# S of the spectral mix: computed in the mix, or beside the forward transform and loaded

## Chip, cores, metric

One Trainium2 chip, one core. The metric is the device time of one launch in microseconds; the median of several runs counts.

## The reference

The input x is (16, 16, 256, 256): 16 images of 16 channels. Layer 0, which holds the change, is a Laplace neural operator on the group-normalized input: with `alpha` the 2D Fourier transform of an image and four complex poles per axis and channel pair (i, k),

```
A  = 1 / (omega1 - weights_pole1)            # (row frequency o, i, k, p)
Bm = 1 / (omega2 - weights_pole2)            # (column frequency x, i, k, q)
S  = einsum('ikpq,oikp,xikq->oxik', weights_residue, A, Bm)
output_residue1 = einsum('biox,oxik->bkox', alpha, S)      # the mix
x1 = ifft2(output_residue1).real
C  = einsum('biox,oikp->bikpx', alpha, A)                  # and a second part by the poles,
D  = einsum('bikpx,xikq->bikpq', C, Bm)                    # which gives x2
x  = x + x1 + x2 / (Nx * Ny)
```

S is the same for all images. Layer 1 (convolutions with a kernel made from the data, Mish, a gate) follows and is not touched.

## The kernel before

Everything is float32. Four stages follow each other: `layer0_forward` (to 1377 us), `layer0_mix` (to 2907), `layer0_back` (to 3560) and `layer1` (to the end).

**Forward.** 64 steps (b, cg): 16 images by 4 groups of 4 channels. A step does `rows` twice (L207 transform along the rows into the PSUM tile `pu`, L214 the part by poles into `pv`), `poles` (L241) and, from the second image on, `columns` for the image before (L313 into the PSUM tile `px`, emptied by ACT at L320 with a scale, sent to the DRAM tensor `al` by DMAs on POOL's queue, L329). `pu` and `px` have two buffers each, of one bank. ACT copies half of `pu` to `right` (L222) and DVE forms sum and difference (L224). `halves` makes the group norm of the next step by two small matmuls (L34, L42) and DVE operations between them. PE's order is the program's, written out by hand; the other engines' order is set by the framework's planner from its own costs, so their work can run ahead of the program where its inputs and buffers allow.

From step 4 on, each step also advances the generator `tables` (L383) by one piece. There are 43: 16 pieces of T, one per output channel k (the residues times Bm: DVE L415 to L431, four matmuls L437, ACT's copy L445, a write to the DRAM tensor `td`), 11 pieces of three groups each of the poles A (DVE L466 to L490, written to `avd`), and 16 of exponentials for the last part (DVE L515 to L534, ACT's Sin L523, written to `ed`).

**Mix.** 33 groups g of four row frequencies. For each: `load_poles` and `load_spectrum` bring A and alpha; `poles` (L629) spreads A into block-diagonal weights `lt`; `residues` (L643) multiplies them with T, which lies in SBUF as `tt`, in 64 matmuls, and S goes from PSUM into the tile `s` by 8 copies on DVE (L651) and 8 on ACT (L653). `spread` (L605 on ACT, L607 on DVE) writes alpha into the tile `alb`, block-diagonal too. `mix` multiplies 256 column frequencies (L665), ACT empties (L672) into `y`. Four times f: `turn` transposes (L681), `columns` goes back along the columns (L700), ACT copies the odd half (L709), DVE forms sum and difference (L712, L713), and POOL's queue writes to `hd` (L720). `s`, `alb` and `y` are single tiles: S and the spread of group g+1 are made in the four turns of group g, after the mix of g has read the old ones, in this order per turn:

```
yt = turn(y, f)
if f == 3: spread(spectrum, f)
for k0 in range(2 if f == 0 else 4 * f, 4 * f + 4, 2): residues(lt, s, k0)
if f < 3: spread(spectrum, f)
if g + 2 < NF: (f == 0: av = load_poles(g + 2)); spectrum[f] = load_spectrum(g + 2, f)
between = columns(g, f, yt)
```

In the mix the order of PE, ACT, DVE and POOL is written out by hand; the loads are issued on SP's queue, in the order in which they stand in the program.

Of the kernel before, what the change touches and what calls it, by code (L numbers as in the profile page):

```python
# [10 lines left out]
F32 = mybir.dt.float32  # L11
# [61 lines left out]
def layer0_forward(ctx, tc, d, al, bd, tabs):  # L73
# [262 lines left out]
    with tc.manual_schedule(engines={mybir.EngineType.PE}):  # L336
# [4 lines left out]
        pieces = tables(ctx, tc, d, psx, tabs)  # L341
        acc = rsc = None
        for i, (b, cg) in enumerate(steps):
# [16 lines left out]
            if b:  # L360
                for g0 in range(8 * cg, 8 * cg + 8 if cg < 3 else NF, 4):
                    columns(b - 1, g0, rsc)
            if i + 2 < len(steps):
                fetched.append(fetch(*steps[i + 2]))
            if i >= 4:
                next(pieces, None)
# [16 lines left out]
def tables(ctx, tc, d, psum, tabs):  # L383

    nc = tc.nc
    td, avd, ed = tabs
# [3 lines left out]

    krow = load(nc, cp, d["krow_t"], [P, N], "krow_t")
    w = frequencies(nc, cp, d["tx"], krow, [P, N], "wt")
# [18 lines left out]
    for k in range(C):  # L411
        e = tp.tile([P, N], F32, tag="te", name="te")
        r = tp.tile([P, N], F32, tag="trec", name="trec")
        br = tp.tile([P, N], F32, tag="tbr", name="tbr")
# [7 lines left out]
        for h in range(2):  # L422
            wt = tp.tile([P, 2, 2, 16, M], F32, tag=f"wt{h}", name="wt")
            shape = [P, 16, M]
            for part, c, coef in ((0, 0, rr), (0, 1, ri), (1, 0, nri), (1, 1, rr)):
                nc.vector.tensor_tensor(
                    wt[:, part, c],
                    mt[:, h].unsqueeze(2).to_broadcast(shape),
                    coef[:, k].unsqueeze(1).to_broadcast(shape),
                    ALU.mult,  # L430
                )  # L431
            wts.append(wt)
        yield
        ps = psum.tile([P, 2, N], F32, tag="px", name="pt")
        for h, wt in enumerate(wts):
            for part, rhs in ((0, br), (1, e)):
                nc.tensor.matmul(  # L437
                    ps[:, h],
                    lhsT=wt[:, part].rearrange("p c i m -> p (c i m)"),
# [4 lines left out]
        t = tp.tile([P, 2, N], F32, tag="tt", name="tt")  # L444
        nc.scalar.copy(t, ps)  # L445
        nc.sync.dma_start(out=td[:, :, k], in_=t)

    krow = load(nc, cp, d["krow_m"], [P, N], "krow_m")  # L450
    w = frequencies(nc, cp, d["ty"], krow, [P, N], "wm")
    sign = load(nc, cp, d["sign_m"], [P, 1], "sign_m")
    pr = cp.tile([P, 32], F32, name="tpr")
    pi = cp.tile([P, 32], F32, name="tpi")
    for q in range(4):
        nc.sync.dma_start(out=pr[32 * q : 32 * q + 32], in_=d["p1r_ip"])
        nc.sync.dma_start(out=pi[32 * q : 32 * q + 32], in_=d["p1i_ip"])
    nc.vector.tensor_scalar(pi, pi, sign, None, ALU.mult)
    pr2 = cp.tile([P, 32], F32, name="tpr2")
    nc.vector.tensor_tensor(pr2, pr, pr, ALU.mult)  # L460
    npr = cp.tile([P, 32], F32, name="tnpr")
    nc.vector.tensor_scalar(npr, pr, -1.0, None, ALU.mult)
    for g in range(NF):
        four = [P, 32, 4]
        e = tp.tile(four, F32, tag="ae", name="ae")
        nc.vector.tensor_tensor(  # L466
            e,
            w[:, 4 * g : 4 * g + 4].unsqueeze(1).to_broadcast(four),
            pi.unsqueeze(2).to_broadcast(four),
            ALU.add,  # L470
        )
        r = tp.tile(four, F32, tag="ar", name="ar")
        nc.vector.tensor_tensor(r, e, e, ALU.mult)
        nc.vector.tensor_tensor(r, r, pr2.unsqueeze(2).to_broadcast(four), ALU.add)
        nc.vector.reciprocal(r, r)
        av = tp.tile([P, 32, 4, 3], F32, tag="av", name="av")
        half = [64, 32, 4]
        nprb = npr.unsqueeze(2)
        nc.vector.tensor_tensor(av[:64, :, :, 1], r[:64], nprb[:64].to_broadcast(half), ALU.mult)
        nc.vector.tensor_tensor(av[64:, :, :, 1], r[64:], e[64:], ALU.mult)  # L480
        nc.vector.scalar_tensor_tensor(
            av[:64, :, :, 0].rearrange("p k f -> p (k f)"),
            e[:64].rearrange("p k f -> p (k f)"),
            -1.0,
            r[:64].rearrange("p k f -> p (k f)"),
            ALU.mult,
            ALU.mult,
        )
        nc.vector.tensor_tensor(av[64:, :, :, 0], r[64:], nprb[64:].to_broadcast(half), ALU.mult)
        nc.vector.tensor_scalar(av[:, :, :, 2], av[:, :, :, 0], -1.0, None, ALU.mult)  # L490
        nc.sync.dma_start(out=avd[g], in_=av.rearrange("p k f l -> p (k f l)"))
        if g % 3 == 2:
            yield


    phase = load(nc, cp, d["phase"], [P, 1], "phase")
    turn = cp.tile([P, 1], F32, name="turn")
    nc.vector.tensor_scalar(turn, phase, TWO_PI, None, ALU.mult)
    last = load(nc, cp, d["last"], [P, 1], "last")
    c1 = 6.28125  # L500
    c2 = float(np.float32(TWO_PI - c1))
    for i, axis in enumerate("12"):
        pr = cp.tile([P, C], F32, name=f"epr{axis}")
        pi = cp.tile([P, C], F32, name=f"epi{axis}")
        for a in range(2):
# [1028 lines left out]
```

## Time and profile before

| | us |
|---|---|
| median of 3 runs (7282.32 to 7289.96) | 7288.94 |
| the profiled execution | 7272.96 |
| its span | 7271.2 |
| forward: from the start to its last ACT copy | 1377.5 |
| mix: to the last group's end | 1529.7 |
| layer0_back, layer1 | 652.8, 3711 |

| engine | busy in the whole span |
|---|---|
| PE (weight loads) | 91% (50%) |
| DVE | 77% |
| ACT | 53% |
| POOL | 48% |

A row of the profile's groups names line, engine, operation, output<-inputs, shapes and count, then busy time and mean duration, then the engine's idle time before these instructions and what ended it. A float32 matmul is recorded as two instructions. A timeline row is start, duration, engine, line, operation, and in brackets the idle time before it. A wait row is the waiting engine and line, the releaser, then the sum in us, the number and the longest.

### The profile page before, as it was taken

The page shows a single profiled execution, that of the slowest core. Times are in us where ns is not written, and L with a number is a line of the kernel's source. Part 1 is how long each engine was busy: PE and PEld are TensorE (multiplying, and loading weights), DVE is VectorE, ACT ScalarE, POOL GpSimd, SP SyncE. Part 2 cuts the span into 40 slices and gives each one's busy share as a digit, 9 for nine tenths or more (in the row PEclk, how much of TensorE's full clock was granted, in tenths as well). Part 3 has the DMA queues.
Part 4 walks back from the last instruction along what each step waited for, and adds up shares of the span by engine and source line. Part 5 has one row for each costly group of instructions (what it writes and reads, how often), then busy time and mean ns, then how long its engine had stood idle before and what let it go on. Part 6 is the DMA issues. An engine that isn't in the chain of part 4 may idle for free.

```text
span 7271.2 us, 144305 instructions
## 1 busy us (share of the span) xinstructions
PE 6603.5 (91%) x55592; PEld 3651.8 (50%) x55592; DVE 5587.6 (77%) x10106; ACT 3876.9 (53%) x6043; POOL 3524.5 (48%) x4614
## 2 busy tenths in 40 slices
PE   7889999899999998999789999999999999999996
PEld 5767778666666766677423333333333333333332
DVE  8999985466666666788678787788877887778875
ACT  2223333466666665222366666666666666666662
POOL 2334445322222222666555666556665566665663
PEclk9899999999999999999889999999999999999999
DMA  3334444433333332999767888888888889888886
GB/s 100 114 112 125 123 120 125 123 99 99 99 96 99 98 99 87 325 325 326 242 180 225 254 269 249 254 261 258 271 244 252 256 254 275 253 247 260 253 261 229
DMA packets 716081, 1443.39 MB, mean 199 GB/s; under 512 B 98954, under 2 KB 525254, under 8 KB 673638
## 3 DMA queue, kind: packets, MB, share of 16 engines
q1 hardware_dynamic: 567206, 959.76, 44.1%
q0 software_dynamic: 148192, 474.40, 21.1%
q8 instruction: 444, 7.27, 0.4%
q14 instruction: 239, 1.96, 0.1%
HBM read 877.12 MB, written 556.47 MB: 197 GB/s over the span
## 4 chain that ended last, share of the span: by engine, by line
PE 37%; DMA 5%; ACT 4%; DVE 3%; issue 1%; POOL 0%; SPq 0%; DVEq 0%; ACTq 0%; POOLq 0%
PE c2ps L1185 14%; PE c L1037 11%; PE pd L1105 10%; ACT wide L1085 3%; DMA rows<-cf 3%; DVE top L1116 1%; PE pr L1064 1%; DMA z<-zn 1%; DVE t L1113 1%; DMA cf<-bot 0%; SPq L1017 0%; DVE pair L1175 0%; ACT L1085 0%; ACT bot L1056 0%; POOL o L1253 0%
## 5 line engine op out<-in xcount | busy, mean ns | idle before, releaser
L1085 ACT ACTIVATE wide<-c,b 32x512 f32<-32x512 f32 x2176 | 1479.0, 680 | 832.1 <-PE c L1037 768.3
L1116 DVE TENSOR_TENSOR top<-pd,t 32x512 f32<-32x512 f32 x2176 | 1504.1, 691 | 53.0 <-DMA cf<-top 0.5
L1037 PE MATMUL c<-z,w 102*128 102x512 f32 x2048 | 1046.0, 636 | 212.3 <-ACT wide L1085 190.8
L1097 POOL COPY wide<-wide 32x1031 f32<-32x1031 f32 (+1 forms) x576 | 576.0, 1000 | 1167.8 <-ACT wide L1085 1141.7
L1113 DVE TENSOR_TENSOR t<-pd,r 64x512 f32<-64x512 f32 x1088 | 744.5, 684 | 504.5 <-PE pd L1105 472.1
L1105 PE MATMUL pd<-wide,dw 128*128 128x512 f32 x2048 | 1026.4, 622 | 16.4 <-DVE top L1116 11.5
L720 POOL DMA_DIRECT2D hd<-h x512 | 324.4, 640 | 1195.9 <-DVE h L713 1170.9
L1037 PEld LDWEIGHTS c<-z,w 102*128 102x128 f32 x2048 | 384.0, 197 | 818.3 <-issue 488.8
L1185 PE MATMUL c2ps<-rows,c 128*32 128x512 f32 x6144 | 722.9, 603 | 24.6 <-DMA rows<-cf 19.0
L1105 PEld LDWEIGHTS pd<-wide,dw 128*128 128x128 f32 x2048 | 370.3, 194 | 641.6 <-issue 490.5
L1098 POOL COPY wide<-wide 32x1031 f32<-32x1031 f32 (+1 forms) x576 | 573.3, 995 | 33.7
L643 PE MATMUL ps<-tt,lt 128*64 128x256 f32 x4224 | 495.5, 384 | 13.8 <-DMA tt<-td 10.6
L700 PE MATMUL ph<-ix,yt 64*128 64x256 f32 x4128 | 500.9, 390 | 5.6 <-issue 4.8
L313 PE MATMUL px<-wxn,u 128*64 128x256 f32 x4224 | 481.7, 379 | 7.8 <-ACT o L320 7.8
L207 PE MATMUL pu<-fy,eo 128*128 128x128 f32 x2048 | 427.0, 292 | 26.5 <-DVE u L224 21.8
L1185 PEld LDWEIGHTS c2ps<-rows,c 128*32 128x32 f32 x6144 | 176.7, 109 | 533.5 <-issue 400.3
L700 PEld LDWEIGHTS ph<-ix,yt 64*128 64x128 f32 x4128 | 392.3, 190 | 92.0 <-issue 45.0
L873 POOL TENSOR_TENSOR x<-x,o 128x512 f32<-128x512 f32 x256 | 324.3, 1267 | 216.6 <-DVE o L872 197.3
L607 DVE TENSOR_SCALAR alb<-alc,m 128x1024 f32<-128x1024 f32 x330 | 420.2, 1398 | 0.0
L214 PE MATMUL pv<-at,eo 128*128 128x128 f32 x2048 | 413.7, 285 | 0.0
L651 DVE COPY s<-ps 128x512 f32<-128x512 f32 x264 | 265.7, 1024 | 189.0 <-PE ps L643 171.2
L665 PE MATMUL pg<-alb,s 128*32 128x64 f32 x16896 | 274.1, 221 | 132.3 <-issue 86.4
(217 smaller groups left out, 11785.6 us busy)
## 6 DMA issues: line engine op xcount, KB each, us to landing
rows<-cf SPq DMA_DIRECT2D x128, 2176.0 KB
z<-zn SPq DMA_DIRECT2D x768, 257.8 KB
cf<-top POOLq DMA_DIRECT2D x512, 240.0 KB, 7.0
cf<-bot POOLq DMA_DIRECT2D x96, 840.0 KB, 11.4
alc<-al SPq DMA_DIRECT2D x264, 256.0 KB
zn<-zb SPq DMA_DIRECT2D x128, 516.0 KB
o<-zn SPq DMA_DIRECT2D x128, 516.0 KB
z<-in_x SPq DMA_DIRECT2D x64, 1024.0 KB
```

What stands on the lines that cost most here:

```text
L207: nc.tensor.matmul(pu[:, xh, e].rearrange("p v m -> p (v m)"), lhsT=lhs, rhs=fy[:, e], start=True, stop=True,)
L313: nc.tensor.matmul(ps[64 * k : 64 * k + 64, :, h], lhsT=u[:, h, part, g0 + j + k].rearrange("p f c -> p (f c)"), rhs=wxn[:, h, part], star ...
L643: nc.tensor.matmul(ps[64 * h : 64 * h + 64, v], lhsT=lt[:, h, k, 1 - v : 3 - v].rearrange("p l f c -> p (l f c)"), rhs=tt[:, h, k], start= ...
L700: nc.tensor.matmul(ph[q][:, e], lhsT=yt[lanes, i].rearrange("p t k -> p (t k)"), rhs=ix[lanes, i], start=n == 0, stop=n == 3,)
L1037: nc.tensor.matmul(ps[:, a], lhsT=w, rhs=z[:k, c : c + 2, 0:N], start=True, stop=True)
L1085: nc.scalar.activation(self.feat[64 - 32 * q : 96 - 32 * q, f, self.groups[g], :H], ps[q][32 * f : 32 * f + 32], AF.Mish, bias=b1[0][32 * ...
L1097: nc.gpsimd.tensor_copy(flat[0:32, f, 1:m], flat[64:96, f, 0 : m - 1])
L1098: nc.gpsimd.tensor_copy(flat[96:128, f, 0 : m - 1], flat[32:64, f, 1:m])
L1105: nc.tensor.matmul(ps, lhsT=dwt if self.tail else dw, rhs=self.feat[:, f, cs, :H], start=True, stop=True,)
L1113: nc.vector.tensor_tensor(t[64:128], ps[:64], self.r[:, cs], ALU.mult)
L1116: nc.vector.tensor_tensor(self.top[32 * f : 32 * f + 32, cs, q], ps[lanes], t[lanes], ALU.add)
L1185: nc.tensor.matmul(ps[32 * j : 32 * j + 32], lhsT=w[:, blk], rhs=src[:, 4 * j + blk : 4 * j + blk + 4, x : x + H], start=(i, blk) == (0, 0 ...
```

## The change

T is no longer kept in DRAM, nor the poles. `tables` now computes S itself: for each pair of output channels (8 pairs), `first` makes T as before for each of the two (into an SBUF tile), `second(k, h)` makes A for 8 of the input channels as a block operand `a` of four quarters of 32 rows each (DVE and ACT), `products` multiplies each quarter of `a` with the same quarter of T, so four operands on 32 rows of the array, each into a PSUM bank of its own, and ACT copies the four banks into `s` tiles (three buffers), each written to the new DRAM tensor `sd` by a DMA on SP's queue. The four banks are the two buffers of `px` and the two of `pu`. `last_products` does the 33rd group, with 64 lanes a bank. One channel pair is 14 pieces, with two exponentials among them 16; 128 in all. They are taken twice a step from the second image on (`columns`, piece, `columns`, piece), three times in the steps with cg = 3. `frequencies` can write in place, and tables share buffers by tags.

In the mix, `poles`, `residues` and T in SBUF are gone. `load_residues_of(g, v)` loads S of a group from `sd` as a tile `raw` of 128 x 4096 (three buffers): once straight (v = 0, one DMA) and once with real and imaginary parts exchanged (v = 1, two DMAs of 64 partitions each). `fill` turns 32 column frequencies of it into `s`: DVE the v = 0 half with a sign per lane, ACT the v = 1 half. Eight fills stand where the eight pairs of `residues` stood. `load_spectrum` is one DMA of 128 partitions instead of two of 64, and lane order and constant masks follow.

```diff
@@ layer0_forward
-        pieces = tables(ctx, tc, d, psx, tabs)
+        pieces = tables(ctx, tc, d, (psx, psu), tabs)
             if b:
                 for g0 in range(8 * cg, 8 * cg + 8 if cg < 3 else NF, 4):
                     columns(b - 1, g0, rsc)
+                    if g0 in (8 * cg, 28):
+                        next(pieces, None)
             if i + 2 < len(steps):
                 fetched.append(fetch(*steps[i + 2]))
-            if i >= 4:
+            if b:
                 next(pieces, None)
@@ tables
+    a = cp.tile([P, 2, 2, 36, 2, 4], F32, name="ta")
+    nc.gpsimd.memset(a, 0.0)
+    def second(k, h):
+        two = [P, 2, 132]
+        e = tp.tile(two, F32, tag="arg", name="ae")
+        nc.vector.tensor_tensor(e, wm..., pi..., ALU.add)
+        r = tp.tile(two, F32, tag="exp_n", name="ar")
+        nc.vector.tensor_tensor(r, e, e, ALU.mult)
+        nc.vector.tensor_tensor(r, r, pr2..., ALU.add)
+        nc.vector.reciprocal(r, r)
+        for v in range(2):
+            t = tp.tile(two, F32, tag="n" if v else "exp_b", name="ax")
+            for j in range(2):
+                nc.scalar.activation(t[:, j], e[:, j], AF.Identity, bias=xc..., scale=xs...)
+            nc.vector.tensor_tensor(t, t, r, ALU.mult)
+            for c in range(2):
+                nc.scalar.activation(a[:, :, c, :33, v], t..., AF.Copy, scale=mc[:, c : c + 1])
+    def banks():
+        return [
+            (psx if r < 2 else psu).tile([P, 2, N], F32, tag="px" if r < 2 else "pu", name="s")
+            for r in range(4)
+        ]
+    def evict(ps, n=P):
+        t = tp.tile([P, 2, N], F32, tag="s", name="s", bufs=3)
+        nc.scalar.copy(t[:n], ps[:n])
+        return t.rearrange("p k x -> p (k x)")
+    def products(k, tt, h, c, g0):
+        ps = banks()
+        for j in range(2):
+            for r in range(4):
+                q = slice(32 * r, 32 * r + 32)
+                nc.tensor.matmul(
+                    ps[r][:, j],
+                    lhsT=a[q, j, c, g0 : g0 + 16].rearrange("p g v f -> p (g v f)"),
+                    rhs=tt[q, h, j], start=True, stop=True,
+                )
+        for r in range(4):
+            dst = sd[g0 : g0 + 16, :, :, 8 * h + 2 * r + c, k : k + 2]
+            nc.sync.dma_start(out=dst.rearrange("g v f k x -> (g v f) (k x)"), in_=evict(ps[r]))
+    def residues():
+        for k in range(0, C, 2):
+            tt = tp.tile([P, 2, 2, N], F32, tag="tt", name="tt")
+            for j in range(2):
+                yield from first(k + j, tt[:, :, j])
+            for h in range(2):
+                second(k, h)
+                yield
+                for g0 in (0, 16):
+                    for c in range(2):
+                        products(k, tt, h, c, g0)
+                        yield
+                last_products(k, tt, h)
+                yield
+    a_steps, b_steps = residues(), exponentials()
+    for i in range(C // 2):
+        for j in range(14):
+            next(a_steps)
+            yield
+            if j in (4, 11):
+                next(b_steps)
+                yield
@@ layer0_mix
+    rp = ctx.enter_context(tc.tile_pool(name="mr", bufs=3))
+    def load_residues_of(g, v):
+        t = rp.tile([P, C, N], F32, tag="raw", name="raw")
+        for lanes, part in ((slice(0, P), None),) if v == 0 else ((slice(0, 64), 1), (slice(64, P), 0)):
+            src = sd[g] if part is None else sd[g, part : part + 1]
+            nc.sync.dma_start(
+                out=t[lanes].rearrange("p k x -> p (k x)"),
+                in_=src.rearrange("v f c k x -> (v f c) (k x)"),
+            )
+        return t
-    def poles(av):
...
-    def residues(lt, s, k0):
...
+    def fill(raw, s, i):
+        xs = slice(32 * i, 32 * i + 32)
+        nc.vector.tensor_scalar(
+            s[:, xs, 0], raw[0][:, :, xs].rearrange("p k x -> p x k"), sg, None, ALU.mult
+        )
+        nc.scalar.copy(s[:, xs, 1], raw[1][:, :, xs].rearrange("p k x -> p x k"))
@@ the loop over groups
+        raw = [load_residues_of(1, v) for v in range(2)]
...
             mix(s, y, between)
             if more:
                 s = gp.tile([P, N, 2, C], F32, tag="s", name="s")
-                residues(lt, s, 0)
+                fill(raw, s, 0)
...
-                    for k0 in range(2 if f == 0 else 4 * f, 4 * f + 4, 2):
-                        residues(lt, s, k0)
+                    for i in range(1 if f == 0 else 2 * f, 2 * f + 2):
+                        fill(raw, s, i)
                     if f < 3:
                         spread(spectrum, f)
                     if g + 2 < NF:
                         if f == 0:
-                            av = load_poles(g + 2)
+                            following = [load_residues_of(g + 2, 0)]
+                        if f == 3:
+                            raw = following + [load_residues_of(g + 2, 1)]
                         spectrum[f] = load_spectrum(g + 2, f)
@@ forward
-        dram.tile([P, 2, C, N], F32, name="td"),
-        dram.tile([NF, P, 384], F32, name="avd"),
+        dram.tile([NF, 2, 4, C, C, N], F32, name="sd"),
```

## Prediction

> **What bounds the kernel now.** I read the busy time by stage first; the stage borders come from the first and last instructions of each stage's tiles.
>
> ```profile
> 137.40:1317.10 1179.70, 1082.49 (x10036) 900.39 (x10034) 992.11 (x2800) 393.09 (x724) 531.91 (x728) 0.97 0.43 118
> 1377.50:1414.40 36.90, 16.29 (x128) 11.12 (x129) 23.83 (x25) 19.88 (x15) 1.11 (x3) 0.76 0.72 251
> 1414.40:2907.20 1492.80, 1359.59 (x26152) 1034.41 (x26152) 995.10 (x1413) 918.71 (x1099) 327.32 (x513) 0.99 0.33 96
> ```
>
> Columns: stretch, length, busy PE, PE weight loads, DVE, ACT, POOL, granted clock, DMA share, GB/s. The change touches the forward transform (to 1377) and the mix (1377 to 2907). In the mix PE is busy 91%, DVE 67%, ACT 62%, DMA a third. In the forward transform PE is busy 92% and DVE 84%; the starts of L231 split it by image: images 1 to 4 take 89.6, 102.2, 103.2 and 99.3 us, images 5 to 12 some 74 to 80, images 13 and 14 69.1 each. The waits of PE there say why:
>
> ```profile
> PE gn_var L42 <- DVE gnq L39: 63.1, 21, 5.4
> PE pu L207 <- DVE u L224: 20.0, 18, 2.0
> PE px L313 <- ACT o L320: 7.2, 4, 1.9
> ```
>
> The tables crowd VectorE early; at 69.1 us an image there are none left, and PE is never idle. ACT almost never holds PE up. For the mix, the groups by form (1500 to 2800, 28.1 of the 33 groups) and the order on PE within one group:
>
> ```profile
> L643 PE MATMUL ps<-tt,lt 128*64 128x256 f32 x3616 | 423.2, 383 | 3.2 <-issue 2.0 <-ACT y L672 1.2
> L607 DVE TENSOR_SCALAR alb<-alc,m 128x1024 f32<-128x1024 f32 x283 | 361.4, 1400 | 0.0
> L605 ACT ACTIVATE alb<-alc,m 128x1024 f32<-128x1024 f32 x169 | 330.7, 2057 | 0.0
> L653 ACT COPY s<-ps 128x512 f32<-128x512 f32 x226 | 232.5, 1029 | 125.0 <-PE ps L643 125.0
> L651 DVE COPY s<-ps 128x512 f32<-128x512 f32 x226 | 227.0, 1023 | 145.9 <-PE ps L643 141.9
> ```
>
> ```profile
> 2006.94 2.89 PE L665 MATMUL pg<-alb,s 128*32 128x64 f32 x192 [1.42 <-DVE s L651]
> ...
> 2020.10 1.95 PE L643 MATMUL ps<-tt,lt 128*64 128x256 f32 x16
> 2021.98 1.10 PE L681 MATMUL pt<-ident,y 128*128 128x128 f32 x8
> 2023.01 1.95 PE L643 MATMUL ps<-tt,lt 128*64 128x256 f32 x16
> 2024.89 3.72 PE L700 MATMUL ph<-ix,yt 64*128 64x256 f32 x32
> 2028.54 1.09 PE L681 MATMUL pt<-ident,y 128*128 128x128 f32 x8
> 2029.56 3.67 PE L643 MATMUL ps<-tt,lt 128*64 128x256 f32 x32
> ```
>
> A group (45.9 us from start to start, the starts of the first L672 of each group) is a mix phase, 2006.94 to 2020.10 = 13.2 us, in which DVE and ACT have little to do since the mix reads `s` and `alb`, single tiles; then four turns of 8.3 us, each 1.1 turn + 3.7 for S + 3.7 columns on PE. S costs PE 4 x 3.7 = 14.7 us a group.
>
> **The Trainium skill.** "TensorEngine Tiling (Array Packing)", Performance Considerations: row tiles of 32 rows run up to four at once, but tiling doesn't speed up the emptying of PSUM. The trace has it for two tiles of 64 rows: 16 matmuls of L700 in 3.72 us, 0.23 each, against 0.43 for two passes of 256 columns. "SBUF — State Buffer", Door 1: a transfer into 64 partitions reaches half of the ports, 196 GB/s at 1 MiB against 328 for 128. The trace's 128-partition load of `tt` ran at 421 GB/s (1385 to 1390), its 64-partition loads of `alc` at 142 (1395 to 1398), with another shape.
>
> **The change, the mix.** It removes L643 (14.7 us of PE), the poles (L629, in DVE's idle mix phase: nothing) and the copies L651/L653; it adds 8 fills on DVE and 8 on ACT, each 128x512, SBUF to SBUF, reading with a stride. No row shows such a read. Bounds for DVE: 0.55 (unstrided) and 1.02 (L651, strided the other way); half a spread (L607, also one strided side), 0.70, is my value. ACT: 0.6 to 1.03, I take 1.03. PE would need only 13.2 + 4 x 1.1 + 3 x 3.7 = 29, so DVE is next. From the end of the mix phase: fill, half of the turn's copy, fill and three spreads end at 6.8; ACT, with its fills and two spreads, frees `odd` at 8.0; the four sums end at 9.4. Turns 1 and 2 then cost 0.65 + 2 x 0.65 + 3 x 1.34 + 4 x 0.36 = 7.4 each (durations less the 0.06 by which neighbours overlap in the trace), turn 3 up to its fills 3.3: 27.5. With the mix phase 40.7.
>
> Then the loads. A group brings 4.2 MB of raw S; DMA is a third busy, so bandwidth is there. But the second half (v = 1, two loads on 64 partitions each) goes into the buffer of the v = 0 half just filled from, so it can start only with the mix phase, and ACT's first fill needs it 13.2 us later. 2.1 MB at the skill's 196 GB/s is 10.7, with issue (2 x 0.35) and about 2 us to land (below) 13.4, beside `hd` writes: an estimated wait of 2 us (0 to 5). Behind the waiting ACT fill stand ACT's turn copy and so PE's columns, so it counts in full. SP itself waits with this load, and behind it stand a spectrum load and the next v = 0 half, both needed a group later: nothing. The one-DMA spectrum load: nothing, it wasn't late. Sum 42.7 against 45.9: **32 x -3.2 = -102 us**, ends 39.5 and 46: -205 to 0. The start of the mix (36.9 us; 4.2 MB of `tt` and S matmuls before, 4.2 MB of raw S and fills after, the same spreads): nothing.
>
> **The change, the forward transform.** The floor is 15 x 69.1 = 1037 us for images 1 to 15; they take 1205 now (143.4 to 1348), so the tables cost 168. Afterwards two or three pieces go into every step of every image, on PE's written order. DVE's table work shrinks a little (33 pole groups of some 3.5 us against 16 `second`s of about as much) and is spread: 38 us an image of its own + about 25, of 69: no bound.
>
> *Products*, 64 pieces: 8 matmuls, 4 at a time, 2 x 0.43 = 0.87 us of PE. They take both `px` banks and both `pu` banks. Between two columns calls: the second `px` bank is emptied 0.95 us after the columns end (0.2 latency + 0.69, L320), and PE, in order, waits. Four banks of 512 then go through ACT at about 0.55 each (L672, 0.59); the next columns wait 0.8 for the first: 2.6 us in all. At the end of a step: 0.87 + 0.95, then the next rows (L207) wait for the third copy, 1.7, and for the fourth, which has only three `s` tiles and so waits until the first DMA has landed: the like-sized `ed` writes land 1.7 to 3.7 us after issue; 0.65 more. 4.2 us in all. Mean 3.4: 218 us. No cover exists: PE had no slack at 69.1. Behind ACT's waiting copy stand `right` and DVE's sums, counted in this. Ends: 1.7 (ACT's order lets half of it vanish) and 4.5.
>
> *Last products*, 16: 0.9 to 1.7 of PE and the same four copies: 3.8, 61 us. *T*, 16: 4 x 0.43 on PE: 29 us. *Exponentials*, 16: 6.6 us an image of four (75.7 - 69.1), as before: 26. *Second*, 16: five DVE passes of 0.35, a reciprocal of 1.8 (L418, 1.74) and eight ACT passes make a chain of some 7 us for one half-step of 10 that DVE shares: 0 to 3 us each, I take 1.5: 25. SP's 256 writes of S, 0.34 each, 69 MB, stand ahead of the input loads, which run two steps ahead; with DMA 43% busy: nothing, up to 2 us an image if SP waits. Sum 359 - 168 = **+190 us** (+23 to +300).
>
> Together +88: the profiled 7273 (7271 span) becomes 7361, and the median, 16 us above it, about **7377 us**.
>
> **Rivals.** *(B) The other side:* the stalls of PE are half as long, because ACT has 60% of its time free and its copies keep up: 1.7 a product piece, 136 + 29 + 26 + 25 - 168 = +48; and raw S is never late: 32 x -5.2 = -166. 7171. It decides as soon as a piece costs under 2.3 us with the mix as I have it (80 x 2.3 + 80 - 168 = 96 against 102). For: today's waits on ACT are 7 us in all. Against: four banks at once on two double buffers. *(C) Raw S is late and fills are dear:* the mix gains nothing and a piece costs 4.5: 360 + 29 + 26 + 50 (3 us a `second`) - 168 = +297; about 7570. For: the 64-partition rows at 142 GB/s. Against: 16 KB rows are longer than those. *(D) The change doesn't do what it says:* four row tiles don't run together, 8 x 0.43 = 3.4 instead of 0.87, + 160: 7540. Against: L700's two run together.
>
> **How the numbers follow.** Chances: forecast 60% (own range 7290 to 7470), B 18%, C 14%, D 8%. Range 7190 to 7540, cutting off the far part of B and C. A measurement tells 0.2% (15 us) from no change: of the forecast's 60%, 4 fall within that and 2 below; so faster 20%, within 4%, slower 76%.
>
> **What would show it.** In the trace after: images 1 to 15 near 93 us each, evenly; PE waiting for ACT's copies of `s` at the columns and at L207, and ACT for the landing of `sd`; groups of the mix near 42.7 with DVE nearly unbroken in the four turns and ACT's first fill waiting for `raw`. Groups at 41 or less refute the late load, images under 85 refute the stalls, and images above 100 mean that tiles run singly or that DVE's chain holds the products.

## The result, and the profile after

The kernel with the change takes **7682.78 us** (median of 4 runs, 7681.56 to 7702.19), the kernel before 7285.63 (4 runs, 7272.75 to 7289.96): ratio 1.0554, 95% interval 1.0533 to 1.0576. The prediction, 7377 us with a range of 7190 to 7540, had the sign, from the forward transform alone, and missed the size by 306 us: for the mix it forecast a gain and there is a loss. The profiled execution took 7702.19 us (span 7700.4, mean granted clock 0.931 against 0.970 before).

The stages first, in the columns of the table that opens the prediction (stretch, length, PE, weight loads, DVE, ACT, POOL, granted clock, DMA share, GB/s). The first row is the forward transform, the second the mix.

```profile
137.40:1671.80 1534.40, 1355.45 (x12108) 1058.90 (x12108) 972.97 (x2613) 628.86 (x1205) 565.62 (x786) 0.92 0.47 134
1709.30:3330.50 1621.20, 1079.45 (x22056) 921.96 (x22056) 808.13 (x1221) 916.02 (x1099) 371.52 (x511) 0.85 0.57 167
```

The first mix matmul starts 295 us later than before (1709.3 against 1414.4). From the first to the last mix matmul it is 1610.7 us against 1482.4, 128 more. What follows differs by 6. So 429 us of span are 295 + 128 + 6, where the prediction had +190 for the forward transform and -102 for the mix. Both stages lost granted clock (0.97 to 0.92, 0.99 to 0.85), and the mix has PE busy only two thirds of the time.

What PE waits for in the forward transform (150 to 1600 us; sum in us, number, longest):

```profile
PE pu L207 <- ACT s L512: 62.6, 55, 4.2
PE px L313 <- ACT s L512: 31.3, 46, 3.7
PE s L521 <- ACT o L320: 27.2, 59, 3.2
PE s L539 <- ACT o L320: 12.6, 15, 2.2
PE gn_var L42 <- DVE gnq L39: 9.4, 6, 2.6
```

The old stall on the group norm (63.1 us) has become 9.4, and ACT's copies have taken its place, as forecast. In the mix (1800 to 3200), by form, with the idle time before and its releasers at the end of each row:

```profile
L762 PE MATMUL ph<-ix,yt 64*128 64x256 f32 x3558 | 504.4, 435 | 166.0 <-DVE yt L749 115.6 <-issue 31.4 <-ACT yt L747 18.9
...
L727 PE MATMUL pg<-alb,s 128*32 128x64 f32 x14336 | 314.0, 260 | 286.8 <-issue 182.7 <-DVE alb L694 102.9 <-ACT odd L771 1.0
...
L715 ACT COPY s<-raw 128x512 f32<-128x512 f32 x223 | 236.2, 1099 | 0.0
L712 DVE TENSOR_SCALAR s<-raw,sg 128x512 f32<-128x512 f32 x222 | 139.9, 662 | 17.5 <-PE pg L727 16.5
```

The fills cost what was estimated (ACT 1.10 us, DVE 0.66) and never wait for `raw` in this stretch. The new row is L727 with 182.7 us of idle time ended by "issue", that is by nothing that the profile shows as a releaser. One mix phase in order of time:

```profile
2209.92 4.07 PE L727 MATMUL pg<-alb,s 128*32 128x64 f32 x160 [3.91 <-DVE alb L694]
2218.84 1.08 PE L727 MATMUL pg<-alb,s 128*32 128x64 f32 x32 [4.86 <-issue]
2219.86 3.78 PE L762 MATMUL ph<-ix,yt 64*128 64x256 f32 x16
2223.57 1.36 PE L727 MATMUL pg<-alb,s 128*32 128x64 f32 x80
2226.43 1.77 PE L727 MATMUL pg<-alb,s 128*32 128x64 f32 x112 [1.50 <-issue]
2228.13 2.00 PE L762 MATMUL ph<-ix,yt 64*128 64x256 f32 x16
2231.12 1.99 PE L727 MATMUL pg<-alb,s 128*32 128x64 f32 x127 [0.99 <-ACT odd L771]
2234.70 0.24 PE L727 MATMUL pg<-alb,s 128*32 128x64 f32 x1 [1.59 <-issue]
```

This phase takes 25 us; the one shown of before took 13.2. The two loads of the exchanged half of S (64 partitions each) run from 2210.4 to 2222.4, and the straight half of a later group follows them directly, from 2222.6 to 2229.9: SP issues it as soon as the loads before it are issued, so all 4.2 MB of a group pass in the mix phase and none in the turns. The trace's DMA records hold the clue to "issue": instructions arrive by DMA too, in packets of 16 KB on a queue of their own. That these are PE's shows in their number, one for 250 matmul and weight-load records both here (423 packets) and in the kernel before (444). Three of them land at 2217.41, 2225.10 and 2233.38, and PE goes on at 2218.84, 2226.43 and 2234.70: 1.43, 1.33 and 1.32 us after each. That is an observation about one group; the experiments test it.

### The profile page after: what moved, and what is told of

It reads as the page before. It is cut to its first block, busy times and chain, and to the rows that moved or that the text cites. A ratio compares the mean times of both kernels' runs of the same rounds, so it can differ in the third digit from the quotient of the medians.

```text
span 7700.4 us, 139663 instructions
## 1 busy us (share of the span) xinstructions
PE 6522.9 (85%) x52904; PEld 3643.9 (47%) x52904; DVE 5368.9 (70%) x9708; ACT 4088.6 (53%) x6491; POOL 3571.0 (46%) x4615
## 4 chain that ended last, share of the span: by engine, by line
PE 50%; DVE 10%; ACT 8%; issue 6%; DMA 5%; POOL 1%; SPq 0%; DVEq 0%; ACTq 0%; POOLq 0%
PE c2ps L1246 13%; PE c L1098 11%; PE pd L1166 10%; PE pg L727 5%; ACT wide L1146 3%; PE ph L762 3%; ACT alb L692 3%; DMA rows<-cf 3%; DVE alb L694 2%; PE py L921 2%; PE py L922 1%; PE pr L1125 1%; DVE top L1177 1%; DVE zb L953 1%; DVE st L938 1%
## 5 line engine op out<-in xcount | busy, mean ns | idle before, releaser
L782 POOL DMA_DIRECT2D hd<-h x512 | 370.3, 730 | 1278.3 <-DVE h L775 1253.1
L762 PE MATMUL ph<-ix,yt 64*128 64x256 f32 x4128 | 584.0, 435 | 192.7 <-DVE yt L749 134.1
L727 PE MATMUL pg<-alb,s 128*32 128x64 f32 x16896 | 370.0, 261 | 363.6 <-issue 204.4
L774 DVE TENSOR_TENSOR h<-ph,odd 128x256 f32<-128x256 f32 x258 | 108.5, 420 | 749.9 <-ACT odd L771 749.9
L762 PEld LDWEIGHTS ph<-ix,yt 64*128 64x128 f32 x4128 | 471.2, 216 | 264.0 <-issue 158.3
L313 PE MATMUL px<-wxn,u 128*64 128x256 f32 x4224 | 510.5, 388 | 35.5 <-ACT s L512 31.3
L727 PEld LDWEIGHTS pg<-alb,s 128*32 128x32 f32 x16896 | 340.1, 138 | 412.6 <-issue 246.0
L207 PE MATMUL pu<-fy,eo 128*128 128x128 f32 x2048 | 454.3, 307 | 76.6 <-ACT s L512 62.6
L329 POOL DMA_DIRECT2D al<-o x544 | 325.5, 611 | 331.0 <-ACT o L320 319.2
L734 ACT COPY y<-pg 128x512 f32<-128x512 f32 x264 | 154.8, 586 | 584.7 <-PE pg L727 584.7
```

The lines of the kernel that those rows point to most:

```text
L207: nc.tensor.matmul(pu[:, xh, e].rearrange("p v m -> p (v m)"), lhsT=lhs, rhs=fy[:, e], start=True, stop=True,)
L313: nc.tensor.matmul(ps[64 * k : 64 * k + 64, :, h], lhsT=u[:, h, part, g0 + j + k].rearrange("p f c -> p (f c)"), rhs=wxn[:, h, part], star ...
L727: nc.tensor.matmul(ps[32 * q : 32 * q + 32, x], lhsT=s[:, i].rearrange("p v k -> p (v k)"), rhs=alb[:, i].rearrange("p j b -> p (j b)"), s ...
L762: nc.tensor.matmul(ph[q][:, e], lhsT=yt[lanes, i].rearrange("p t k -> p (t k)"), rhs=ix[lanes, i], start=n == 0, stop=n == 3,)
```

## Experiments

Each kernel but the last ran once and is set beside 7683 us (after) or a run of the kernel before on the same chip (7280 to 7296). The change's own four runs lie 21 us apart, so a difference of some 20 us in the time alone says nothing; the stages and the waits then have to tell. The change's profiled run is the slowest of its four, so differences from its stages are rather too large. "Mix phase" is from the first to the last start of a group's 512 mix matmuls, "turns" from there to the next group, both as means; "images" are means over images 0 to 14, split by the starts of L231 as in the prediction; "half-clock time" is the sum of the clock records with half of the full clock. Before: group 45.9 us = 14.5 phase + 31.4 turns. After: 49.85 = 24.2 + 25.8 (means over slightly different groups).

**Theory 1:** the loads of raw S delay PE's instructions, which stretches the mix phase. The rivals are that the change's own order does it, or the length of the DRAM rows. **Theory 2:** in the forward transform the four bank copies set the price of a piece, and PE's pauses lower the granted clock. The rivals are SP's queue, which holds back the writes of S, and ACT as the single copier.

**No loads.** Raw S is loaded for the first two groups only; the later groups use it again.

```diff
-                        if f == 0:
-                            following = [load_residues_of(g + 2, 0)]
-                        if f == 3:
-                            raw = following + [load_residues_of(g + 2, 1)]
```

> The changed kernel without its loads of S from the third group on: every later group is filled from the tiles of group 1, so S is wrong for it and nothing else changes. Theory I (the loads of raw S run through the mix phase, and PE's own instructions, which come by DMA in 16 KB packets, come late behind them): the mix phase falls from 25 us to 13 to 15, a group from 49.1 to about 40, the whole to about 7380 (7350 to 7430). Theory II (S's matmuls are gone from the four turns, PE pauses there, its granted clock is halved, and the mix phase is slow for that; the loads are innocent): the mix phase stays above 20 us, a group above 46, the whole above 7590.

Measured: 7422.85 us; group 41.5 = 15.1 + 26.3. The group is within 0.8 us of the prediction's 40.7 without a late load, in part by luck: the phase is 1.9 us longer than its 13.2 and the turns 1.2 shorter than its 27.5. Without loads the mix would gain 4.4 us a group; all that it lost comes with the loads.

**Rows of 4 KB.** The same loads, each split into four DMAs of four channels.

```diff
-            nc.sync.dma_start(...)
+            src = src.rearrange("v f c k x -> (v f c) k x")
+            for k in range(0, C, 4):
+                nc.sync.dma_start(out=t[lanes, k : k + 4], in_=src[:, k : k + 4])
```

> The changed kernel with each load of raw S cut into four by output channel, so that a descriptor is 4 KB instead of 16. The same bytes at the same time. Theory I: an instruction packet stands behind shorter ones; the mix phase falls to 15 to 20 us, the whole by 130 to 250. Theory II: nothing moves by more than 30.

Measured: 7663.8 us; mix phase 22.8. Shorter rows give back 1.4 us of the 9.1 that the loads add to a phase, so the length of a row is not the main cause.

**Which half.** Two kernels: the exchanged half (v = 1) loaded once only; and the exchanged half loaded as one DMA of 128 partitions, without the exchange.

```diff
-    rp = ctx.enter_context(tc.tile_pool(name="mr", bufs=3))
+    rp = ctx.enter_context(tc.tile_pool(name="mr", bufs=2))
-        t = rp.tile([P, C, N], F32, tag="raw", name="raw")
+        t = (cp if v else rp).tile([P, C, N], F32, tag=f"raw{v}", name="raw")
...
-                            raw = following + [load_residues_of(g + 2, 1)]
+                            raw = following + raw[1:]
```

> The exchanged half of S (v=1, two loads on 64 partitions) is loaded once, not for each group, so S is wrong from the second group on; the straight half is loaded as before. Theory (the two 64-partition loads in the mix phase hold up PE's instructions): mix phase 15 to 16 us as without any load, group near 41.5, time near 7425. Rival (all bytes count, the straight half as much): mix phase near 19.5, group near 45.5, time near 7550.

```diff
-        for lanes, part in ((slice(0, P), None),) if v == 0 else ((slice(0, 64), 1), (slice(64, P), 0)):
+        for lanes, part in ((slice(0, P), None),):
```

> The second half is loaded as one DMA of 128 partitions, without the exchange of real and imaginary parts (so S is wrong); bytes and place in the order stay. Theory (the 64-partition form[...] is what holds up PE's instructions): mix phase 16 to 19 us, group 42 to 44, time 7480 to 7560. Rival (any 2 MB in the mix phase do it): mix phase 22 to 24, time within 40 us of 7683.

Measured: 7496.39 and 7548.56 us; mix phase 18.2 and 20.2, group 43.8 and 45.65. Both phases lie between the two expectations: the straight half alone already costs 3.1 us a phase over none, the second 2 MB cost 2.0 as a 128-partition load and 6.0 as two 64-partition loads. So bytes count, and the form of the exchanged load triples its share. In both kernels, as in the change, what is loaded goes through in the mix phase. The waits of L727 for its instructions (1800 to 3000 us) climb the same ladder; first no loads, then the straight half, then both on 128 partitions, then the change:

```profile
PE pg L727 <- issue: 40.0, 40, 2.0
```

```profile
PE pg L727 <- issue: 90.6, 53, 3.7
```

```profile
PE pg L727 <- issue: 119.3, 52, 5.4
```

```profile
PE pg L727 <- issue: 158.2, 50, 7.6
```

The number rises in the first step only, from 40 to 53, while the sum goes up fourfold, although fewer groups fall into the same 1200 us: mainly the waits get longer. Set against the instruction packets (1800 to 2900 us, pauses over 0.5 us before the mix matmuls that end 1.1 to 1.7 us after a packet has landed):

| raw S loaded | pauses | mean, us | sum per group, us | mix phase, us |
|---|---|---|---|---|
| none | 28 | 1.25 | 1.3 | 15.1 |
| straight half | 41 | 1.90 | 3.1 | 18.2 |
| both, 128 partitions | 45 | 2.38 | 4.5 | 20.2 |
| the change | 43 | 3.27 | 6.4 | 24.2 |

Nearly every "issue" pause is in the table: all 28, 41 and 45 of the first three kernels, and 42 of 43 in the change. Packets land some 0.11 to 0.13 times a us here, so a moment taken at random would lie in a stretch of 0.6 us behind a landing in about 7 of 100 cases. The kernel before has such pauses too, 2.2 us a phase (30 pauses, 53 us, 24 groups); the prediction took them as a fixed part of the phase.

**The same load on the kernel before.** The first attempt added DRAM-to-DRAM copies of the table T to each group. They depended on nothing:

```diff
+                        if f == 3:
+                            for h in range(4):
+                                nc.sync.dma_start(
+                                    out=tabs[3][h], in_=tabs[0][32 * h : 32 * h + 32].rearrange("p t k x -> (p t) (k x)")
+                                )
```

> The kernel before, with one thing added: in each group from the turn f = 3 on, four DRAM-to-DRAM copies of 1 MB in 16 KB rows, for which nobody waits. Theory I: the mix phase grows from 13.2 us to 18 or more, with PE waiting for nothing that the profile shows, and the whole by 150 to 350. Theory II: PE's turns are as full as before, so the mix phase stays at 13 to 14 and the whole within 30 of the kernel before.

Measured: 7330.27 us, but inconclusive: all these copies were issued between 564 and 1615 us, most of them under the forward transform; only 23 of 124 came after the start of the mix. The second attempt ties 2 MB to each mix phase: a write of a quarter of `alb` that the next spread waits for.

```diff
+                        if f == 3:
+                            for h in range(2):
+                                nc.sync.dma_start(
+                                    out=tabs[3][h],
+                                    in_=alb[64 * h : 64 * h + 64, :64].rearrange("p x j b -> p (x j b)"),
+                                )
```

> The kernel before, with 2 MB more to move in each mix phase: after the last spread of a group, two DMAs of 64 partitions write a quarter of alb to DRAM (16 KB a row; nobody reads it), and the next spread waits for them. Theory (a 64-partition transfer in the mix phase holds up PE's instructions, whatever else the change does): mix phase from 14.5 to 18 to 24 us, time +100 to +290 us. Rival (the stretched phase comes from the change's own order, its fills or its spectrum load): mix phase within 1 us of 14.5, time within 40 us.

Measured: 7451.47 us, +156 over the kernel before; mix phase 20.3, turns 31.4 as ever. One of its phases:

```profile
2086.98 1.13 PE L700 MATMUL ph<-ix,yt 64*128 64x256 f32 x8
2092.87 2.08 PE L700 MATMUL ph<-ix,yt 64*128 64x256 f32 x8 [4.76 <-issue]
2094.88 2.95 PE L665 MATMUL pg<-alb,s 128*32 128x64 f32 x120
```

The same place in the kernel before, without the write:

```profile
2009.76 1.13 PE L700 MATMUL ph<-ix,yt 64*128 64x256 f32 x8
2011.64 1.13 PE L700 MATMUL ph<-ix,yt 64*128 64x256 f32 x8 [0.75 <-issue]
```

And all waits of the mix matmuls on "issue" from 1850 to 3000 us, first before, then with the write:

```profile
PE pg L665 <- issue: 51.6, 31, 4.3
```

```profile
PE pg L665 <- issue: 119.9, 35, 8.3
```

The kernel before, its matmuls untouched, shows the change's symptom, and its phase grows by 5.8 us for 2 MB on 64 partitions, where the exchanged half cost 6.0. Theory 1 holds without any other part of the change, and with a write to DRAM instead of a load.

**Moving half of the bytes into the turns.** Raw S in six tiles of half the columns, so that part of it is loaded in the turns.

```diff
-    rp = ctx.enter_context(tc.tile_pool(name="mr", bufs=3))
+    rp = ctx.enter_context(tc.tile_pool(name="mr", bufs=6))
...
+                        if f == 1:
+                            following[1] += [load_half_of(g + 2, 1, 0)]
                         if f == 3:
-                            raw = following + [load_residues_of(g + 2, 1)]
+                            raw = [following[0], following[1] + [load_half_of(g + 2, 1, 128)]]
```

> Raw S in tiles of half the columns, six of them, so that half of the exchanged part is loaded in the turns and only half in the mix phase; the bytes are the same, rows are 512 B in DRAM. Theory (what counts is how much is moved while PE fetches the mix's instructions): mix phase 24.2 to 19 to 22, turns up to 1 us longer, time 7540 to 7640. Rival (bytes count wherever they are moved, or 512 B rows cost more): group 49.5 or more, time 7680 to 7800.

Measured: 7594.96 us; mix phase 20.75, turns 25.75, not longer. Of the packets of raw S, 42% now fall in the turns, where the change has none, and where PE runs some 130 of a group's 672 matmul records. So the same bytes cost less where PE has few instructions to bring in: 88 us in all. Place and row length changed together here, 512 B instead of 16 KB; rows of 4 KB alone gave 1.4 us a phase, against 3.4 now, so most of the gain is put down to the place, which no run shows by itself.

**The exchange on the chip.** No exchanged load; ACT and POOL fill the second half from the straight tile, across partitions.

```diff
-        for lanes, part in ((slice(0, P), None),) if v == 0 else ((slice(0, 64), 1), (slice(64, P), 0)):
+        for lanes, part in ((slice(0, P), None),):
...
-        nc.scalar.copy(s[:, xs, 1], raw[1][:, :, xs].rearrange("p k x -> p x k"))
+        nc.scalar.copy(s[:64, xs, 1], raw[0][64:, :, xs].rearrange("p k x -> p x k"))
+        nc.gpsimd.tensor_copy(s[64:, xs, 1], raw[0][:64, :, xs].rearrange("p k x -> p x k"))
...
-                            raw = following + [load_residues_of(g + 2, 1)]
+                            raw = following
```

> No exchanged load at all: ACT and POOL fill the v=1 half, 64 partitions each, from the other half of the straight tile. The output is the reference's. Theory (the mix loses its gain only by the second load): group near 44 as without that load, time near 7500. Rival (POOL, with the writes of hd in its order and a strided read, comes late with its fills): turns 28 to 35 us, time 7600 to 7850.

Measured: 7651.13 us; mix phase 18.3 as expected without the exchanged load, but turns 30.2. The fills in it:

```profile
L712 DVE TENSOR_SCALAR s<-raw,sg 128x512 f32<-128x512 f32 x188 | 256.1, 1394 | 11.4 <-issue 11.0
L716 POOL COPY s<-raw 64x512 f32<-64x512 f32 x188 | 251.2, 1370 | 0.0
```

DVE's unchanged fill takes 1.39 us on average instead of 0.66, and the mean hides two cases: of the 264 fills of this run, 110 had no POOL copy beside them and took 0.69 us, the other 154 took 1.92, the longest 3.5, through two POOL copies in a row. PE's wait for DVE's turned tile grows with it, from 99 to 145 us in about as many groups. The Trainium skill, "SBUF — State Buffer", "Who interferes with whom", says that DVE and GpSimd share a pair of SBUF ports which one instruction at a time can hold, and that the other then stands still. Fills that last through whole POOL copies agree with that; but the page has it only for DVE instructions that use both of their ports, and whether this fill does isn't shown.

**One operand instead of four**, in the forward transform: one bank, one copy, sent four times.

```diff
-            for r in range(4):
+            for r in range(1):
...
-        for r in range(4):
-            dst = ...; nc.sync.dma_start(out=..., in_=evict(ps[r]))
+        t = evict(ps[0])
+        for r in range(4):
+            dst = ...; nc.sync.dma_start(out=..., in_=t)
```

> The changed kernel with one operand of 32 rows in each products piece instead of four: one bank, one copy by ACT, and the same four writes from that one tile; three quarters of S are left out. Theory of the stalls (PE waits for px and pu banks that ACT has yet to empty, and the clock falls with the gaps): images 1 to 15 fall from 101 us to 80 to 86, the whole by 230 to 310. Rival (the cost is in DVE's chain for the operands, in the exponentials and in SP's order): images stay above 94, the whole falls by less than 100.

Measured: 7507.03 us, -176; images 87.2 us instead of 99.2, between the two expectations. A piece between two columns calls takes 1.16 us of PE's time, waits included, against 2.68. So the four banks and their copies, which this run doesn't separate, are most of a piece's price; what the images still lacked to the floor was left to explain.

**Another queue; another copier.** The writes of S on POOL's queue; and two of the four copies on DVE.

```diff
-            nc.sync.dma_start(out=dst.rearrange("g v f k x -> (g v f) (k x)"), in_=evict(ps[r]))
+            nc.gpsimd.dma_start(out=dst.rearrange("g v f k x -> (g v f) (k x)"), in_=evict(ps[r]))
... (the writes of `last_products` likewise)
```

> The writes of S go on POOL's queue instead of SP's. Theory (SP holds the writes back: it waits 231 us for exponentials before an input load, and ACT waits 132 us for the landing of writes of S): images fall from 99 to some 93, the time by 60 to 100 us. Rival (ACT's four copies one after the other are the bound, the queue doesn't matter): within 20 us of 7683. POOL's queue also carries the writes of the column transform, so images of over 105 mean that these hold S up instead.

```diff
-    def evict(ps, n=P):
+    def evict(ps, n=P, eng=nc.scalar.copy):
...
-            nc.sync.dma_start(out=dst.rearrange("g v f k x -> (g v f) (k x)"), in_=evict(ps[r]))
+            nc.sync.dma_start(out=dst.rearrange("g v f k x -> (g v f) (k x)"),
+                in_=evict(ps[r], P, nc.vector.tensor_copy if r > 1 else nc.scalar.copy))
```

> Two of the four bank copies of each piece go to DVE. Theory (four copies in a row on ACT hold PE): each of 80 pieces is up to 1.1 us shorter, the time falls by 40 to 90 us. Rival (DVE, in an order of the planner's own, comes to them late): PE then waits for DVE at the rows, images stay at 99 or grow, up to +80 us.

Measured: 7698.47 and 7696.66 us, images 101.7 and 100.0: neither helps. With the other queue ACT's waits for the landing of S fall from 132 to 90 us, but the writes of `al`, on the same queue, now stand with them. With DVE as second copier two new waits take the place of the old one:

```profile
PE pu L207 <- DVE gnq L36: 53.0, 26, 5.8
...
PE pu L207 <- DVE s L512: 41.6, 27, 4.5
```

PE now waits for DVE's copies, and again for the group norm, whose operations stand on DVE too. Whether more copiers would help if they came in time stays untested. My reading of SP's waits as a cause of the longer images is not borne out by the first of the two.

**Keeping PE busy.** Two matmuls whose result nobody uses follow each products piece.

```diff
+        spare = psn.tile([P, N], F32, tag="gn", name="spare")
+        for n in range(2):
+            nc.tensor.matmul(spare, lhsT=w[:, :P], rhs=w, start=True, stop=True)
```

> After each of the 64 products pieces PE gets two more matmuls of 128 x 256 into the bank of the group norm's sums (0.43 us each, the result unused), just where it would wait for ACT's copies. Without an effect on the clock they lie in waits or add at most 64 x 0.87 = 56 us. Theory (the forward transform's missing 90 us are PE's pauses, which bring the granted clock down to a half): half-clock time before the mix from 257 to 120 to 200 us, images from 99 to 95 to 98, time 7620 to 7670. Rival (the clock doesn't follow pauses as short as these): half-clock time stays at 230 to 280 us, images 99 to 103, time 7680 to 7740.

Measured: 7669.57 us; half-clock time before the mix 117 instead of 257 us, images 98.2. The stages (same columns), from 143 us to the start of image 15, of the change and of this kernel:

```profile
143.00:1559.00 1416.00, 1246.27 (x11086) 974.16 (x11084) 941.60 (x2514) 590.03 (x1135) 510.91 (x702) 0.92 0.48 137
```

```profile
143.00:1542.00 1399.00, 1260.84 (x11328) 971.59 (x11329) 940.89 (x2511) 587.96 (x1134) 510.98 (x700) 0.97 0.49 139
```

The unused matmuls take 74 us of PE's time, yet PE is busy only 15 us longer, at a clock of 0.97, and the stretch is 17 us shorter. Images stayed just above the expected 95 to 98, since the waits shrank by 32 us only. How much of this is noise can be read from the seven other kernels here that have the change's forward transform as it is: from the first matmul of image 1 to the last of the columns they take 1521 to 1532 us, with 201 to 232 us at half clock (the change 1530 and 232). This kernel takes 1511 with 92, and the last one below, with the same unused matmuls, 1522 with 130. So the clock follows PE's pauses, clear of noise; that the time falls is not shown, only that 74 us of added work cost none.

**The same in the turns of the mix**, ahead of the real columns:

```diff
+        for q in range(2):
+            nc.tensor.matmul(ph[q][:, 0], lhsT=ident, rhs=ix[:, q], start=True, stop=True)
```

> In each of the four turns of a group PE gets two more matmuls of 128 x 256 (0.43 us each) into the column banks, ahead of the real ones that overwrite them, where it would wait 1 to 2.5 us for the turned tile yt. Without an effect on the clock they are hidden or add up to 4 x 0.87 x 32 = 111 us. Theory (PE's pauses in the turns, 9.2 us a group, lower the clock, and the mix phase then runs longer: 16.7 us busy against 13.6 without loads): half-clock time in the mix from 484 to 200 to 330 us, mix phase 24.2 to 21 to 23, time 7590 to 7650. Rival (the pauses for the instructions themselves lower it): half-clock time stays above 430, time 7670 to 7790.

Measured: 7657.58 us; half-clock time in the mix 382 instead of 484 us, turns 24.8 instead of 25.8, mix phase 24.1, unchanged. (Four other kernels with the change's mix have 30 to 40 us less at half clock than the change's profile, so some 60 us of the 102 are sure.) A miss for the theory as stated: filling the turns' pauses makes the turns faster, but not the phase, where the pauses for instructions remain.

**All that helped, together:** halves, and both fillers.

> All that helped and leaves the output the reference's: raw S in halves, two more matmuls after each products piece, two more in each turn. If the three add up: 7683 - 88 - 13 - 60 = about 7520, still 3% above the kernel before, since the forward transform keeps some 270 us of what S costs there. If the clock is the common cause, they overlap, and it stays at 7550 to 7600.

Measured: 7557.9 us (median of 4 runs, 7548.3 to 7569.05), ratio to the kernel before 1.0378 (1.0353 to 1.0403). Better than the change by 125 us; the single gains (88, 13 and 25) add up to 126. The time lies in the range expected for overlapping gains, but gains that add up show no overlap, and 13 and 25 are hardly clear of noise. It is still slower than before, because images 1 to 15 keep 284 of the change's 291 extra us in its profiled run (7569.05). No version here beats the kernel before.

## Why the prediction was wrong, point by point

Two steps failed. For the mix, the prediction took a phase of 13.2 us as unchanged by the loads that run beside it; it became 24.2, and a group 49.85 us instead of 42.7, which is 229 us over the 32 groups. For the forward transform, it took the floor of 69.1 us an image over to a kernel with pauses; images 1 to 15 cost 291 us more than before instead of 190.

**Forward: the pieces were right, the clock was missing.** PE's time over images 1 to 15 (143 us to the last image's columns), from the trace, overlaps taken out, in us:

| | before | predicted | after | one operand | PE kept busy |
|---|---|---|---|---|---|
| matmuls of the transform itself | 1073 | 1037 | 1146 | 1089 | 1090 |
| T | 31 | 29 | 31 | 31 | 31 |
| products, last products (and fillers) | - | } 330 | 142 | 96 | 213 |
| PE idle | 97 | } with waits | 173 | 96 | 141 |
| sum | 1201 | 1396 | 1492 | 1311 | 1474 |
| half-clock time | 82 | | 232 | 92 | 92 |

The prediction's 218 + 61 + 26 + 25 = 330 for products, last products, exponentials and `second` met 142 + 173 = 315. A piece between columns takes 2.68 us (predicted 2.6). One at the end of a step takes 2.9, and the 74 us of idle time at L207 belong to these 34 pieces and to waits of an older kind (24 us before): 1.5 to 2.2 more each, so 4.4 to 5.1 for a predicted 4.2. The term that failed is the **floor of 69.1 us an image**: it was read from two images without pauses, at a clock of 1.00, and stands for the same matmuls in 1037 us; they took 1146. The 109 us are close to half of the 232 at half clock, 116. The other columns agree: 36, 52 and 53 us over the floor against halves of 41, 46 and 46. One place shows it, at the end of a step with a products piece:

```profile
814.68 0.80 PE L207 MATMUL pu<-fy,eo 128*128 128x128 f32 x2 [1.66 <-ACT s L512]
...
816.55 0.63 PE L207 MATMUL pu<-fy,eo 128*128 128x128 f32 x2
816.98 0.64 PE L214 MATMUL pv<-at,eo 128*128 128x128 f32 x2
...
822.02 0.39 PE L214 MATMUL pv<-at,eo 128*128 128x128 f32 x2
822.25 0.39 PE L207 MATMUL pu<-fy,eo 128*128 128x128 f32 x2
```

After a wait of 1.66 us pairs start 0.43 us apart; seven us later 0.22 to 0.23. The clock records have half of the clock from 813.99 to 820.82. The clock's price is this second half of a stall, and the sum priced stalls only once. The Trainium skill has both halves of it: "TensorE: Matmul & The Clock Gate", Part 1, tells of a half-rate clock after an idle window of about 3.4 us, and "A second HAM failure mode: psum-queue depth-cycling" of short pauses between groups of matmuls that suffice. Here the second describes it: of PE's 173 us of idle time over images 1 to 15, in 210 pauses, only three pauses are over 3.4 us, 12 us together, and the half-clock stretches before the mix rose from 18 to 37.

**SP's writes** ("nothing, up to 2 us an image"): ACT does wait 132 us for landings of S, but with the writes on another queue nothing is gained. Nothing here speaks against the value, though the other queue brought waits of its own.

**Mix: the fills and the DVE chain were right, the load was put in the wrong place.** Turns were forecast at 27.5 and took 25.8; the fills 0.70 and 1.03, they took 0.66 and 1.10. The step "the mix phase 13.2" failed, 24.2 measured, and with it "DMA is a third busy, so bandwidth is there". Of the 11.0 us, 1.3 are that the one phase it read is shorter than the mean of 14.5, 0.6 come without any load, and 9.1 with the loads. The load does run beside the mix phase, and is in time: ACT's first fill never waits for it (in the phase shown it landed 13 us ahead), so the 2 us put down there were 0. But it delays the packets that bring PE's instructions. Of a phase's PE time, without loads 13.6 us are busy and 1.55 idle; with the change 16.7 and 7.7. So of 9.2 us that the loads add, 6.1 are pauses, shown to be late instructions by their ladder and by the kernel before with an added write; 3.1 are matmuls running slower, at a half-clock time in the mix of 484 us against 252 without loads. Which pauses lower it was only half settled: filling those in the turns took 60 to 100 us off the half-clock time and left the phase as it was.

Per transfer, the Trainium skill, "SBUF — State Buffer", Door 1, has half of the ports and so about half of the rate on 64 partitions. The trace agrees packet by packet, 1.23 us for 16 KB of the exchanged half against 0.61 for the straight one; the 2.1 MB took 12.1 us against 7.4 as means over 22 groups. The ladder adds what it means for a neighbour: 6.0 us a phase against 2.0. Why the instruction packets come late isn't shown: their own transfer is hardly longer (mean 1.18 us, 1.10 without loads), so they wait before it, but no record tells where.

**Rivals.** *B* (stalls halved, raw never late) had the second half right and still failed. *C* came nearest in time, 7570 (7586 with the 16 us that the forecast adds for the median), by causes that did not occur, so by luck: raw S was not late, and a piece between columns did not cost 4.5. *D* is refuted: four row tiles start 6 to 7 ns apart (805.193, 805.199, 805.206 and 805.213 us). **The range** left out what none of the cases held: a cost to PE itself of traffic that nobody waits for, and the clock.

## What to carry to other kernels

A matmul phase with many short instructions needs its instruction stream, and the stream comes by DMA like the data: in this kernel large transfers belonged where PE runs few, long matmuls, and on 128 partitions rather than 64. Waits on "issue" in such a phase should be set against the instruction packets before a load is priced at nothing. Price a stall of PE with the clock it costs afterwards, here about half of the time spent at half clock; a floor measured without pauses isn't the floor of the new kernel. Work moved off a busy engine into a stage whose PE has no slack (69.1 us an image with no idle time) was paid there in full, with the PSUM banks that it borrows.

## What the runs showed of the hardware that was not expected

- In the change's mix PE resumed 1.2 to 1.7 us after a 16 KB instruction packet had landed, in 42 of 43 pauses on "issue" before mix matmuls; such pauses grew from a mean of 1.25 to 3.27 us with 4.2 MB a group more to load, and with a 2 MB write added to the kernel before the longest wait on "issue" before mix matmuls grew from 4.3 to 8.3 us.
- Pauses of PE far below the 3.4 us of the skill's page went with a halved clock: 232 us at half clock over images 1 to 15, with three of 210 pauses over that length. Unused matmuls in these pauses, 74 us of PE's time, brought it to 92 us and did not lengthen the stage.
- A 64 x 512 copy on POOL made the DVE fills beside it take 1.92 us on average, up to 3.5, instead of 0.69.
